# Message passing on 100,000 edges: seven edge splits in place of six, and who seeds and ends the last pass

## The chip, the cores and the metric

The kernel runs on 1 core of one Trainium2 chip. The metric is the device time of one execution in microseconds. Before the change it is 1114.98 us, the median of 3 runs (1113.57 to 1116.06). A profile was taken of one further execution; its times are counted from the first instruction.

## The reference

There are 6250 nodes with 128 features and 100,000 edges sorted by `dst`. Each edge makes a message from its two nodes and its own features, the messages are normed and cut at zero, and they are summed at `src` (which is in random order); then the nodes are normed.

```python
msg_in = concatenate([x[src], x[dst], edge_attr], axis=-1)      # 100000 x 384
h = msg_in @ W + b                                              # 100000 x 128
h = (h - mean(h)) * rsqrt(var(h) + 1e-5) * gamma + beta
msg = relu(h)
out = segment_sum(msg, src, num_segments=6250)
x = layernorm(x + out)
```

## The kernel before, in words

**Tiles and slots.** The edges are 782 tiles of 128. Four tiles make a *slot*; there are 196 slots, q = 0 to 195. The loop at the end of `fast_path` goes over the slots. In each slot TensorE forms the part of `h` that comes from the edge's features and from `x[dst]` (L619 and L623, into `hp`), ScalarE copies it out of the accumulators into a staging tile `hs` (`evict`, L633; a small copy at L568 adds one more column for three slots at a time), and GpSimd writes the tile's 128 rows into a table in HBM (`scatters`, L650), one indirect DMA for each tile, so 782 in all. The row to which an edge goes was worked out before by `places` (DVE, some TensorE and ScalarE work, in 20 pieces spread over the slots up to about 176). Staging has room for nine slots (`HS = 9`): ScalarE can be at most about that far ahead of GpSimd, and L568 is where it waits for room.

**Splits.** `scatters` sorts the edges by `src`: 50 blocks of 125 nodes. The edges come in splits, each with a table of its own in HBM. The list `SPLITS` holds for each split the number of tiles, k (each block has room for k x 128 edges), f (rows from f on are filled with neutral rows beforehand, `clear`, by DMAs from `empty`), and the sizes of the pieces of `places`. If a block of a split gets more than k x 128 or fewer than f edges, the program leaves the fast path for `general_path`. The number of tiles processed after sorting is 50 k for each split, filled or not.

**Items.** Once all edges of a split lie in its table, the split is taken in 25 pairs of blocks. An *item* is one pair (`n = 1`), or two pairs (`n = 2`, for splits with k = 2); an item has 2 k n tiles, handled in groups of at most four (k = 3: two groups of three; k = 4 and two-pair items: two groups of four; a single pair of k = 2: one group of four). For an item, `FLOW` lists these steps with an offset each: load `hl` (L725, SP), one-hot rows `ohe` (L748, DVE), their transposes (L760, TensorE) and the copy of them `ohn` (L764, ScalarE); for each group a copy of the rows into an accumulator (`seed`, L770, ScalarE), products that add `x[src]` (`pick`, L787, TensorE), squares (L796) and one root (L799) on ScalarE, a reciprocal (L805) and the norm with the cut at zero (L811) on DVE; for each pair the sums over edges (L820, TensorE, into `pa`) and their addition to `acc` (L826, DVE). Four work steps go with each item, so items follow each other at four steps' distance. `steps_due(q)` says how many steps are to have been done by slot q: the 25 items of a split are spread evenly over the slots between the end of that split plus 5 slots (`LAG`) and the end of the next split plus 5. The order on each engine is thus fixed in the program; GpSimd's scatters of a slot are tied to products of the following slot.

**The last split** has no later slots to hide behind. Its 25 pairs are taken as 14 *units* (sizes 1, eleven times 2, 1, 1) by the class `Unit` in `tail`, which also ends the nodes: `begin`, `stats`, `var`, `norm`, `end` give the final norm, and `end` issues the DMA that writes a unit's nodes out. A unit's `seed` is a product with the identity on TensorE (L876) or a copy on ScalarE (L874). The last four units a, b, c, d are ended by hand behind the loop. `end` takes two GpSimd instructions (L972, L973), or one DVE instruction for each block (L976) where its argument says so.

Of the kernel before, what the change touches and what calls it, by code (L numbers as in the profile page):

```python
# [12 lines left out]
AF = mybir.ActivationFunctionType  # L13
# [11 lines left out]
NB, BN = 50, 125  # L25
# [10 lines left out]


SPLITS = [(168, 4, 320, [12, 24, 44, 44, 44]),
          (168, 4, 320, [42, 42, 42, 42]),
          (168, 4, 320, [42, 42, 42, 42]),  # L40
          (120, 3, 192, [40, 40, 40]),
          (80, 2, 128, [40, 40]),
          (78, 2, 128, [39, 39])]
EARLY = 19
TMAX = 44
BY_PE = 4
# [24 lines left out]
def col_bc(t, n):  # L71

    return t.unsqueeze(2).to_broadcast([t.shape[0], t.shape[1], n])
# [7 lines left out]
def flat(t):  # L81
    return t.rearrange("p t d -> p (t d)")


def fast_path(ctx, tc, io, bad_d, found):
# [3 lines left out]
    nc = tc.nc  # L89
# [157 lines left out]
    bias = const.tile([P, D], F32, name="bias")  # L247
# [587 lines left out]
    class Unit:  # L835
# [130 lines left out]
            nc.vector.scalar_tensor_tensor(self.shift[:, :m], self.total[:, :m], -1.0 / D,  # L966
                                           self.frstd[:, :m], op0=ALU.mult, op1=ALU.mult)

        def end(self, last=False):
            y, m = self.y, self.m  # L970
            if not last:
                nc.gpsimd.tensor_tensor(y, y, col_bc(self.frstd[:, :m], D), op=ALU.mult)  # L972
                nc.gpsimd.tensor_tensor(y, y, col_bc(self.shift[:, :m], D), op=ALU.add)  # L973
            else:
                for j in range(m):
                    nc.vector.tensor_scalar(y[:, j, :], y[:, j, :], self.frstd[:, j:j + 1],  # L976
                                            self.shift[:, j:j + 1], op0=ALU.mult, op1=ALU.add)
            nc.sync.dma_start(io["out"][:, self.b0 * D:(self.b0 + m) * D], flat(y))


    n_split = len(SPLITS)
# [95 lines left out]
    TWINS = 8  # L1077
    pairs, first_item = [], []
    for s in range(n_split - 1):
        n = TWINS if s == n_split - 2 else 0  # L1080
        first_item.append(len(pairs))
        pairs += [(s, p, 2) for p in range(0, 2 * n, 2)]
        pairs += [(s, p, 1) for p in range(2 * n, NB // 2)]
# [31 lines left out]
    def work(n):  # L1115

        nonlocal n_steps
        for _ in range(n):
            for off, step in FLOW:
                i = n_steps - LEAD - off  # L1120
                if i % 4 or not 0 <= i // 4 < len(pairs):
                    continue
                if step is None:
                    load_pairs(*pairs[i // 4])
                    continue
                if off == 0:
                    at_work[i // 4] = Pairs(i // 4, *pairs[i // 4])
                step(at_work[i // 4])
            n_steps += 1
# [9 lines left out]
    def steps_due(q):  # L1139
        for (q0, n0), (q1, n1) in zip(due, due[1:]):  # L1140
            if q0 <= q < q1:
                return n0 + (n1 - n0) * (q - q0) // (q1 - q0)
        return 0
# [12 lines left out]
    for s, (n_tiles, _, _, _) in enumerate(SPLITS):  # L1156
        p0, p1 = first_tile[s] // PT, -(-first_tile[s + 1] // PT)
        slots = p1 - p0
        for i in range(slots):
# [16 lines left out]
            n = steps_due(q + 1) - n_steps  # L1176
# [25 lines left out]
    units = [Unit(sum(sizes[:i]), n) for i, n in enumerate(sizes)]  # L1202
    n = len(units)
# [49 lines left out]
    work(1)  # L1253
    units[0].turned()
    work(1)
    units[0].pick(0)
    units[1].ones()
    work(2)
    units[1].turn()
# [12 lines left out]
    a, b, c, d = units[-4:]  # L1272
# [21 lines left out]
    c.var()  # L1294
    for u in (b, d, c):
        u.norm()
        u.end(u is not b)
    order.close()


@with_exitstack
def gnn_resnorm_kernel(ctx, tc, io):
    nc = tc.nc
    keep = ctx.enter_context(tc.tile_pool(name="keep", bufs=1))
    bad_t = keep.tile([1, 1], I32, name="bad_t")
    with ExitStack() as inner:
        found = []
        fast_path(inner, tc, io, bad_t, found)
    with tc.If(found[0] > 0, preferred_fallthrough_block=True, label="general"):
        with ExitStack() as inner:  # L1310
            general_path(inner, tc, io)
# [233 lines left out]
```

## Time and profile before

| | |
|---|---|
| median of the runs | 1114.98 us |
| the profiled execution's own time | 1118.29 us |
| its span, first to last instruction | 1116.5 us |
| mean granted TensorE clock | 0.904 of full speed |
| busy: TensorE / DVE / ScalarE / GpSimd | 868.9 / 846.0 / 754.6 / 798.5 us |
| moved by DMA | 247.20 MB, 221 GB/s over the span |

A row of a timeline has the start in us, the duration in us, the engine, the line, the operation, output <- inputs, the shape, the count, and in brackets the idle time of the engine just ahead of it with what ended that. In a table by windows each row has the window, its length, the busy time of the engine with the number of instructions, then the granted clock, the share of the DMA engines and GB/s. In a table of waits, the numbers are the total in us, how often, and the longest. The names of engines are PE (TensorE), DVE (VectorE), ACT (ScalarE), POOL (GpSimd) and SP (SyncE); L650 is a line of the kernel above. "issue" is idle time for which the profile shows no wait.

### The profile page before, as it was taken

Reading aid. Unit: us, or ns where it says so; the run is one execution under the profiler, and the core shown is the slowest. Engines: PE = TensorE matmul, PEld = TensorE weight load, DVE = VectorE, ACT = ScalarE, POOL = GpSimd, SP = SyncE. Lnnn points to the kernel's source line nnn. Section 1 sums busy time; section 2 is a strip of 40 time slices with the busy share of each in tenths; the row PEclk is TensorE's granted clock in tenths of the full one; section 3 lists DMA queues with packets and bytes.
Section 4 is the critical chain, followed back from the end, with each engine's and each line's share of the span. In section 5 each row is a group of like instructions: output and inputs, shape, how many; then the busy total and the mean of one; then the engine's idle time right before and its main releaser. Section 6 shows DMA issues by size and latency. Waiting matters only on the chain. (4 is left out here: it accounts for less than half of the span.)

```text
span 1116.5 us, 27245 instructions
## 1 busy us (share of the span) xinstructions
PE 868.9 (78%) x8880; PEld 805.1 (72%) x8880; DVE 846.0 (76%) x2364; ACT 754.6 (68%) x2983; POOL 798.5 (72%) x832
## 2 busy tenths in 40 slices
PE   6758656454887688788868688888989899987994
PEld 3657546444887678788868688887978788976773
DVE  7874656634687587768777687988898988877997
ACT  4324422115776667567767678887988999987995
POOL 2677777777777777777777777777777777774264
PEclk7788897666999899878989899998999999999998
DMA  7799999546787666667877648876877767744331
GB/s 218 230 274 267 287 312 295 185 157 205 246 282 223 218 207 204 224 205 242 277 236 239 209 147 290 268 228 223 256 245 241 232 200 248 250 144 136 124 122 61
DMA packets 128050, 247.20 MB, mean 221 GB/s; under 512 B 47005, under 2 KB 61231, under 8 KB 127897
## 3 DMA queue, kind: packets, MB, share of 16 engines
q1 hardware_dynamic: 101924, 191.92, 56.0%
q0 software_dynamic: 25104, 53.05, 13.3%
q8 instruction: 71, 1.16, 0.5%
q14 instruction: 81, 0.66, 0.2%
q10 hardware_dynamic: 870, 0.40, 0.1%
HBM read 155.49 MB, written 89.80 MB: 220 GB/s over the span
## 5 line engine op out<-in xcount | busy, mean ns | idle before, releaser
L650 POOL DMA_INDIRECT sorted<-hs,place_i x782 | 758.1, 969 | 251.0 <-issue 94.2
L787 PE MATMUL sel<-xa,ohn 128*128 128x128 bf16 x2550 | 189.1, 226 | 107.1 <-ACT sel L770 105.9
L619 PE MATMUL hp<-w,eT 128*128 128x128 f32 x1564 | 240.5, 303 | 22.0 <-ACT hs L633 22.0
L619 PEld LDWEIGHTS hp<-w,eT 128*128 128x128 f32 x1564 | 218.7, 214 | 53.0 <-issue 27.2
L787 PEld LDWEIGHTS <-ohn 128*128 128x128 bf16 x2550 | 165.4, 101 | 118.3 <-issue 99.8
L811 DVE SCALAR_TENSOR_TENSOR msg<-sel,rstd,cut 128x128 f32<-128x128 f32 x850 | 240.5, 345 | 7.9
L820 PE MATMUL pa<-msg,ohe 128*128 128x130 f32 x1700 | 231.3, 288 | 15.3 <-DVE acc L826 8.6
L796 ACT ACTIVATE sq<-sel 128x128 f32<-128x128 f32 x850 | 224.4, 282 | 27.8 <-PE sel L787 27.6
L820 PEld LDWEIGHTS pa<-msg,ohe 128*128 128x128 f32 x1700 | 210.8, 199 | 20.2 <-DVE acc L826 10.2
L796 ACT ACTIVATION_READ_ACCUMULATOR sq<-sel 128x1 f32 x850 | 180.9, 213 | 0.0
L748 DVE TENSOR_TENSOR ohe<-hl,beside 128x1024 f32<-128x1024 f32 (+2 forms) x117 | 130.2, 1113 | 21.4 <-DMA hl<-sorted 10.5
L633 ACT COPY hs<-hp 128x512 f32<-128x512 f32 x196 | 113.4, 580 | 43.5 <-PE hp L623 36.5
L770 ACT COPY sel<-hl 128x512 f32<-128x512 f32 (+1 forms) x225 | 128.1, 569 | 15.9 <-DVE msg L811 15.6
L568 ACT COPY hs<-sloc 128x12 f32<-128x12 f32 x66 | 14.1, 213 | 161.3 <-DMA sorted<-hs,place_i 158.7
L607 DVE TENSOR_SCALAR ohd<-db,part_w 128x512 bf16<-128x512 bf16 x192 | 69.1, 361 | 61.4 <-DMA db<-drel_d 47.2
L764 ACT COPY ohn<-tr 128x1024 bf16<-128x1024 bf16 (+2 forms) x117 | 107.8, 921 | 5.3 <-PE tr L760 5.3
L805 DVE RECIPROCAL rstd<-std 128x4 f32<-128x4 f32 (+1 forms) x225 | 38.2, 170 | 80.8 <-ACT std L799 79.7
L826 DVE TENSOR_TENSOR acc<-acc,pa 128x260 f32<-128x260 f32 x125 | 52.3, 418 | 54.4 <-PE pa L820 54.3
L623 PE MATMUL hp<-win,ohd 126*128 126x128 bf16 x782 | 82.0, 231 | 1.1 <-DMA win<-xb_d 1.1
L799 ACT ACTIVATE std<-ss,eps 128x4 f32<-128x4 f32 (+1 forms) x225 | 66.9, 297 | 7.3
L760 PE MATMUL tr<-ident_h,ohe 128*128 128x128 bf16 x850 | 69.4, 225 | 2.4 <-issue 2.0
L623 PEld LDWEIGHTS <-ohd 126*128 126x128 bf16 x782 | 66.2, 105 | 5.1 <-issue 1.4
(199 smaller groups left out, 1033.9 us busy)
## 6 DMA issues: line engine op xcount, KB each, us to landing
eT<-in_eT SPq DMA_DIRECT2D x96, 512.0 KB
hl<-sorted SPq DMA_DIRECT2D x75, 528.0 KB
db<-drel_d SPq DMA_DIRECT2D x96, 256.0 KB
sorted<-empty SPq DMA_DIRECT2D x100, 198.0 KB
hl<-sorted SPq DMA_DIRECT2D x50, 264.0 KB
sorted<-hs,place_i POOLq DMA_INDIRECT x782
hl<-sorted SPq DMA_DIRECT2D x25, 396.0 KB
sorted<-empty SPq DMA_DIRECT2D x50, 132.0 KB
```

The lines of the kernel that those rows point to most:

```text
L619: pe(nc.tensor.matmul(hp[:, j, :], eT[:, at], w[:, 2, :], start=j == 0, stop=False, skip_group_check=True), 4)
L623: pe(nc.tensor.matmul(hp[:, j, :], oh[:3 * WN, at], win[:3 * WN, :], start=False, stop=j == m - 1, skip_group_check=True))
L633: nc.scalar.copy(hs[:, :m, 0:D], hp[:, :m, :])
L650: i = nc.gpsimd.indirect_dma_start(out=sorted_d[s][:, :], out_offset=bass.IndirectOffsetOnAxis(ap=place_i[:parts, t:t + 1], axis=0), in_=h ...
L748: nc.vector.tensor_tensor(self.ohe[:, :k, :], self.hl[:, :k, D:D + 1].to_broadcast([P, k, P]), row_bc(iota_p, k), op=ALU.is_equal)
L760: pe(nc.tensor.transpose(tr[:, j, :], half[:, j0 + j, 1::2], ident_h))
L764: nc.scalar.copy(self.ohn[:, :self.k, :], self.tr[:, :self.k, :])
L770: nc.scalar.copy(self.sel[g][:, :m, :], self.hl[:, j0:j0 + m, 0:D])
L787: pe(nc.tensor.matmul(sel[:, j, :], self.ohn[:, j0 + j, :], xa[:, b, i * D:(i + 1) * D], start=False, stop=j == m - 1 and i == 2, skip_gro ...
L796: nc.scalar.activation(sq[:, j, :], self.sel[g][:, j, :], AF.Square, accum_out=ss[:, j:j + 1])
L811: nc.vector.scalar_tensor_tensor(self.msg[:, j0 + j, 0:D], self.sel[g][:, j, :], rstd[:, j:j + 1], cut, op0=ALU.mult, op1=ALU.max)
L820: pe(nc.tensor.matmul(self.pa[:, h, :], self.ohe[:, i * k + j, :], self.msg[:, i * k + j, :], start=(j == h), stop=(j == k - 2 + h)), 4)
```

## The change

The list of splits has seven entries. The sum of k over the splits is 19 in both versions, the last split has k = 2 in both, and so 850 sorted tiles are taken as items and 100 as units in both. The fifth split (k = 2) is taken as twelve two-pair items and one single; the sixth, like the fifth before, as eight two-pair items and nine singles. There are 130 items in place of 117 and 250 groups in place of 225. The first unit's seed moves from TensorE to ScalarE. Of the last three units, b is ended by DVE in place of GpSimd, d by ScalarE in place of DVE, and c by DVE as before.

```diff
 SPLITS = [(168, 4, 320, [12, 24, 44, 44, 44]),
-          (168, 4, 320, [42, 42, 42, 42]),
-          (168, 4, 320, [42, 42, 42, 42]),
-          (120, 3, 192, [40, 40, 40]),
+          (124, 3, 192, [42, 42, 40]),
+          (124, 3, 192, [42, 42, 40]),
+          (124, 3, 192, [42, 42, 40]),
           (80, 2, 128, [40, 40]),
-          (78, 2, 128, [39, 39])]
+          (80, 2, 128, [40, 40]),
+          (82, 2, 128, [42, 40])]
...
-        def end(self, last=False):
+        def end(self, last=None):
             y, m = self.y, self.m
-            if not last:
+            if last is nc.scalar:
+                for j in range(m):
+                    nc.scalar.activation(y[:, j, :], y[:, j, :], AF.Identity,
+                                         bias=self.shift[:, j:j + 1],
+                                         scale=self.frstd[:, j:j + 1])
+            elif last is None:
                 nc.gpsimd.tensor_tensor(y, y, col_bc(self.frstd[:, :m], D), op=ALU.mult)
                 nc.gpsimd.tensor_tensor(y, y, col_bc(self.shift[:, :m], D), op=ALU.add)
             else:
...
-        n = TWINS if s == n_split - 2 else 0
+        n = 0 if SPLITS[s][1] > 2 else TWINS if s == n_split - 2 else NB // 4
...
-    units[0].pick(0)
+    units[0].pick(0, nc.scalar)
...
     for u in (b, d, c):
         u.norm()
-        u.end(u is not b)
+        u.end(nc.scalar if u is d else nc.vector)
```

How the items lie over the slots, from `steps_due` with each list (an item of n pairs has 2 k n tiles):

| before: slots | items of split | tiles a slot | after: slots | items of split | tiles a slot |
|---|---|---|---|---|---|
| 47 to 89 | 1st | 4.8 | 47 to 78 | 1st | 6.5 |
| 89 to 131 | 2nd | 4.8 | 78 to 109 | 2nd | 4.8 |
| 131 to 161 | 3rd | 6.7 | 109 to 140 | 3rd | 4.8 |
| 161 to 181 | 4th | 7.5 | 140 to 160 | 4th | 7.5 |
| | | | 160 to 180 | 5th | 5.0 |
| 181 to 190 | 5th, two-pair | 7.1 | 180 to 190 | 6th, two-pair | 6.4 |
| 190 to 197 | 5th, single | 5.1 | 190 to 197 | 6th, single | 5.1 |

The first place is ScalarE's queue between its copy of slot 173 into staging and that of slot 174, where `hs` is the staging tile, and `sel`, `sq` and `std` are the seed, squares and root of a group (the numbers are those of the buffers). Before the change:

```order
L770 COPY sel_12973<-hl_12689 128x384
L796 ACTIVATE sq_12976,ss_12975<-sel_12917 128x128 x3
L799 ACTIVATE std_12980<-ss_12975,eps_100 128x3
L764 COPY ohn_12956<-tr_12957 128x768
L770 COPY sel_13006<-hl_12783 128x384
L796 ACTIVATE sq_13009,ss_13008<-sel_12973 128x128 x3
L799 ACTIVATE std_13013<-ss_13008,eps_100 128x3
L770 COPY sel_13064<-hl_12783 128x384
L796 ACTIVATE sq_13067,ss_13066<-sel_13006 128x128 x3
L799 ACTIVATE std_13071<-ss_13066,eps_100 128x3
L568 COPY hs1_194<-sloc_164 128x12
L633 COPY hs1_194<-hp_13050 128x4x128
```

After the change, the same engine between the copies of the same two slots (its lines stand one further on):

```order
L765 COPY ohn_13566<-tr_13567 128x1024
L771 COPY sel_13644<-hl_13322 128x512
L797 ACTIVATE sq_13647,ss_13646<-sel_13606 128x128 x4
L800 ACTIVATE std_13652<-ss_13646,eps_101 128x4
L569 COPY hs1_197<-sloc_165 128x12
L634 COPY hs1_197<-hp_13669 128x4x128
```

Three groups of three tiles stood there between two slots, and one group of four stands there now; the other groups went to earlier slots.

The second place is the beginning of the last pass on ScalarE: `ohn` is the first unit's copied transposes, followed by the last item's squares. Before:

```order
L867 COPY ohn<-tr 128x512
L796 ACTIVATE sq,ss<-sel 128x128 x4
L799 ACTIVATE std<-ss,eps 128x4
L898 ACTIVATE sq,ss_15466<-sel 128x128 x4
L901 ACTIVATE std_15472<-ss_15466,eps 128x4
```

And now:

```order
L868 COPY ohn<-tr 128x512
L797 ACTIVATE sq,ss<-sel 128x128 x4
L800 ACTIVATE std<-ss,eps 128x4
L875 COPY sel<-hl 128x512
L899 ACTIVATE sq,ss_15856<-sel 128x128 x4
```

The seed stands behind the last item's squares and root, and the product L876 that made it is gone from TensorE's queue at that place.

The third place is the end of DVE's queue: `frstd` and `shift` belong to the final norm of b (4 blocks), d and c (2 each), in that order. Before:

```order
L964 RECIPROCAL frstd<-fstd 128x4
L966 TENSOR_SCALAR shift<-total,frstd 128x4
L964 RECIPROCAL frstd<-fstd 128x2
L966 TENSOR_SCALAR shift<-total,frstd 128x2
L976 TENSOR_SCALAR y<-y,frstd,shift 128x128 x2
```

And now:

```order
L965 RECIPROCAL frstd<-fstd 128x4
L967 TENSOR_SCALAR shift<-total,frstd 128x4
L982 TENSOR_SCALAR y<-y,frstd,shift 128x128 x4
L965 RECIPROCAL frstd<-fstd 128x2
L967 TENSOR_SCALAR shift<-total,frstd 128x2
```

DVE's four instructions for b come in ahead of d's norm, and d's two leave DVE: ScalarE's queue now ends with them (L974).

## The prediction

> **What bounds the kernel now.** I read the engines' totals first, then GpSimd's scatters by stretch, then ScalarE's waits for staging, then the table by stages, then the last 15 us. The totals point at no engine:
>
> ```profile
> PE 868.9 (78%) x8880; PEld 805.1 (72%) x8880; DVE 846.0 (76%) x2364; ACT 754.6 (68%) x2983; POOL 798.5 (72%) x832
> ```
>
> The scatters, taken by their line in two stretches, tell more (duration min/median/max in ns, then first and last start):
>
> ```profile
> L650 POOL DMA_INDIRECT sorted<-hs,place_i x481: 963/967/1128, 277.5 to 889.0; - x161
> L650 POOL DMA_INDIRECT sorted<-hs,place_i x102: 868/967/1068, 890.3 to 1024.4; - x102
> ```
>
> In the first stretch 480 intervals take 611.5 us, 1.274 us each, with hardly a deviation: GpSimd goes at its own pace, 5.10 us for a slot of four, and sets the time. In the second, 101 intervals take 134.1 us; at 1.274 they would take 128.7. So GpSimd lost **5.4 us** after 890 us, and the timeline says where and to whom:
>
> ```profile
> 908.41 0.97 POOL L650 DMA_INDIRECT sorted<-hs,place_i  x1 [1.92 <-PE pa L820]
> ...
> 1005.57 0.97 POOL L650 DMA_INDIRECT sorted<-hs,place_i  x1 [0.96 <-ACT sq L796]
> ...
> 1010.08 0.97 POOL L650 DMA_INDIRECT sorted<-hs,place_i  x1 [2.28 <-PE pa L820]
> ...
> 1024.40 0.87 POOL L650 DMA_INDIRECT sorted<-hs,place_i  x1 [0.30 <-issue]
> ```
>
> The usual gap is 0.30; here the other engines were late with what the scatters wait for. Behind the last scatter stand its landing, the loads of the first units, and a dense last pass:
>
> ```profile
> 1026.54 15.29 SPq L847 DMA_DIRECT2D hl<-sorted  x13
> 1029.23 0.69 DVE L854 TENSOR_TENSOR ohe<-hl,beside 128x512 f32<-128x512 f32 x1 [0.95 <-DMA hl<-sorted]
> ```
>
> ```profile
> 1050.00:1100.00 50.00, 48.31 (x459) 37.25 (x458) 48.34 (x209) 45.84 (x243) 30.05 (x29) 1.00 0.30 101
> ```
>
> DVE waits for the data at 1029.23, so the pass starts when the scatters let it; after that PE and DVE are busy 48 us in 50. The program therefore has two parts: scatters until 1025.3 (1024.40 + 0.87), then 91.2 us to the span's end at 1116.5, with 100 tiles in both versions.
>
> Why was GpSimd starved only late? ScalarE's waits for staging room, in 240 to 440, 440 to 655 and 655 to 830 us, one row each (there is no such row from 830 to 945):
>
> ```profile
> ACT hs L568 <- DMA sorted<-hs,place_i: 53.9, 11, 14.7
> ...
> ACT hs L568 <- DMA sorted<-hs,place_i: 52.5, 14, 6.2
> ...
> ACT hs L568 <- DMA sorted<-hs,place_i: 2.8, 2, 2.0
> ```
>
> and the copies into staging (x is slots) in the stages:
>
> ```profile
> 240.00:440.00 200.00, 21.75 (x38) 0.87 0.74 237
> 440.00:655.00 215.00, 24.83 (x43) 0.89 0.71 226
> 655.00:830.00 175.00, 18.54 (x32) 0.98 0.74 238
> 830.00:945.00 115.00, 11.57 (x20) 1.00 0.72 228
> 945.00:990.00 45.00, 5.20 (x9) 1.00 0.74 239
> 990.00:1018.00 28.00, 2.32 (x4) 1.00 0.38 110
> ```
>
> By the counts these are the first to fourth splits' items, then the two-pair items and the singles. The engines' own need for a slot is the window less the wait, over the slots: (200 - 53.9)/38 = 3.84 us and (215 - 52.5)/43 = 3.78 at 4.8 tiles a slot; (175 - 2.8)/32 = 5.4 at 6.7 tiles; 115/20 = 5.75 at 7.5; 45/9 = 5.0 at 7.1; 28/4 = 7.0 for the singles. Against GpSimd's 5.10, the first two stages have over a microsecond a slot to spare and the third and fourth are too slow. The engines enter 655 us with staging full, lose 32 x 0.3 = 10 us and, up to the stall at 908, some 14 slots x 0.65 = 9 us. A full lead is thus worth about **19 us** of falling behind.
>
> **The change part by part.** *The splits.* The 850 tiles before the last pass stay, and the dense end thins: slots 131 to 190 had 6.7, 7.5 and 7.1 tiles a slot, slots 109 to 190 get 4.8, 7.5, 5.0 and 6.4. By the needs above (between 3.8 at 4.8 tiles and 5.4 at 6.7 I take 5.2 for 6.5): slots 47 to 78 lose 31 x 0.1 = 3 us of lead, 78 to 140 win it back at over 1 us a slot, 140 to 160 lose 20 x 0.65 = 13 us of the 19, 160 to 180 win about 20 x 1.1, again full. The two-pair stage is no denser than the 5.0 us one of before; the singles lose 7 x 1.9 = 13 us, and that too is within the 19. So no stall after 890 us should remain: between 0 and -5.4 us. I take **-5.0**, near the full end, since 13 of 19 leaves room only if the lead is really full.
>
> What the split adds: 25 more groups and 25 more additions, and groups of three in place of four.
>
> ```profile
> L770 ACT COPY sel<-hl 128x512 f32<-128x512 f32 x175 | 103.9, 594 | 13.7 <-DVE msg L811 13.7
> L770 ACT COPY sel<-hl 128x384 f32<-128x384 f32 x50 | 24.2, 484 | 2.2 <-DVE msg L811 2.0
> L799 ACT ACTIVATE std<-ss,eps 128x4 f32<-128x4 f32 x175 | 52.1, 297 | 5.7
> L805 DVE RECIPROCAL rstd<-std 128x4 f32<-128x4 f32 x175 | 29.7, 170 | 75.2 <-ACT std L799 74.9
> L826 DVE TENSOR_TENSOR acc<-acc,pa 128x260 f32<-128x260 f32 x125 | 52.3, 418 | 54.4 <-PE pa L820 54.3
> ```
>
> ScalarE: seeds 100 x 0.594 + 150 x 0.484 = 132.0 against 128.1, and 25 roots x 0.297 = 7.4, so 11 us; DVE: 25 x (0.418 + 0.170) = 14.7 us. Spread over 150 slots this is 0.1 us a slot, hidden by the microsecond to spare in slots 78 to 140 and 160 to 180; in the dense stage the need of 5.75 already has groups of three. Without that cover it would be up to 15 us. Fills grow by 25 DMAs of 132 KB and loads by 25 issues on SP: 3.3 MB beside 247.2, in stages whose DMA share is 0.71 to 0.74. I take 0.
>
> *The last three units.*
>
> ```profile
> 1106.69 0.17 DVE L966 SCALAR_TENSOR_TENSOR shift<-total,frstd 128x4 f32<-128x4 f32 x1
> 1107.03 0.17 DVE L964 RECIPROCAL frstd<-fstd 128x2 f32<-128x2 f32 x1 [0.17 <-ACT fstd L958]
> 1107.23 0.56 DVE L966 SCALAR_TENSOR_TENSOR shift<-total,frstd 128x2 f32<-128x2 f32 x1
> 1107.83 1.40 DVE L976 TENSOR_SCALAR y<-y,frstd,shift 128x128 f32<-128x128 f32 x2
> 1109.15 0.15 DVE L964 RECIPROCAL frstd<-fstd 128x2 f32<-128x2 f32 x1
> 1109.60 0.60 DVE L976 TENSOR_SCALAR y<-y,frstd,shift 128x128 f32<-128x128 f32 x2
> ```
>
> ```profile
> 1107.85 1.04 POOL L973 TENSOR_TENSOR y<-y,shift 128x512 f32<-128x512 f32 x1
> ```
>
> d's two instructions took 1.40 us and c's 0.60: while POOL works on b (to 1108.89), DVE is slow. With b on DVE, four instructions from 1106.86 take 1.2 us, the norms of d and c 0.45 each (1109.15 to 1109.60), c's two 0.60: 1109.55 in place of 1110.20. ScalarE's two for d come from 1108.5; such an operation is not in the trace, its bounds are nothing and the 0.33 us step at which L976 goes times two plus a start, under c's end either way. The DMA of c is then late next. Between 0 and -1.0; I take **-0.7**. Nothing is queued behind d's instructions on ScalarE.
>
> *The first unit's seed.*
>
> ```profile
> 1032.07 1.02 PE L876 MATMUL sel<-hl,ident 128*128 128x512 f32 x2
> 1032.08 0.30 ACT L799 ACTIVATE std<-ss,eps 128x4 f32<-128x4 f32 x1
> 1032.93 0.83 PE L887 MATMUL sel<-xa,ohn 128*128 128x128 bf16 x12
> ```
>
> It now waits behind that root: 1032.38 plus 0.59 for such a copy is 1032.97, where the picks began at 1032.93. Queued behind the picks on PE are the second unit's transposes and the last item's sums. Nothing won or lost: 0.
>
> *A cold restart of PE.* With a lead of 6 us or more at slot 195, PE has finished the items and stands idle some 7 us until the last scatters have landed; before, it was busy up to the end. What that costs shows at 250 us:
>
> ```profile
> 259.85 1.44 PE L787 MATMUL sel<-xa,ohn 128*128 128x128 bf16 x12 [11.15 <-ACT sel L770]
> 261.08 1.06 PE L760 MATMUL tr<-ident_h,ohe 128*128 128x128 bf16 x8
> 261.93 2.02 PE L619 MATMUL hp<-w,eT 128*128 128x128 f32 x8
> 265.00 1.14 PE L619 MATMUL hp<-w,eT 128*128 128x128 f32 x8
> 266.20 0.83 PE L787 MATMUL sel<-xa,ohn 128*128 128x128 bf16 x12
> ```
>
> After 11.15 us idle, twelve picks take 1.44 in place of 0.83 and eight f32 products 2.02 in place of 1.14; some 4 us later all is fast again. At the restart stand four transposes (+0.2), eight f32 sums (+0.9, half hidden, since PE no longer has the seed) and twelve picks (+0.6), ahead of an addition for which DVE waits. Between 0 and +2; I take **+1.0**. The Trainium skill, "TensorE: Matmul & The Clock Gate", section "What's actually happening", states that an idle window of about 3.4 us halves the clock and a busy one restores it, and the rows above agree (1.44 over 0.83, for about 4 us). By this rule alone any idle gap over 3.4 us ahead of the last pass costs the restart, and without it the sum below would be 1 us less.
>
> *Sum:* -5.0 - 0.7 + 0 + 1.0 = -4.7 us. The profiled execution took 1118.29 (its span 1116.5 and 1.8 around it), so it would take 1113.6; it lies 3.3 above the median of the runs, and the same step from the median gives 1114.98 - 4.7 = **1110.3 us**.
>
> **The rivals.** *The stall only moves.* The stage at 7.5 tiles a slot is still there, at slots 140 to 160. It needs 13 us of lead; if splits' beginnings keep the lead at slot 140 under that, GpSimd loses it there instead, and a scatter lost early is as lost as a late one. Against: 62 light slots stand ahead, and the waits of 53.9 and 52.5 show how much is spare at 4.8 tiles. Price: the 5.0 comes back, 1115.3; without the idle gap 1114.3. I call it 1114.5.
>
> *Slower, by slots 47 to 78.* They get 6.5 tiles a slot, where the clock was 0.87 in place of 0.98. The stage decides from 5.10 + 19/31 = 5.7 us a slot on. At 6.0 it loses 28 us, of which 19 are lead: 9 us of stall, 1110.3 + 9 = 1119. For it: PE's cold rows above stand just there. Against:
>
> ```profile
> 240.00:440.00 200.00, 148.66 (x1563) 143.12 (x1564) 141.22 (x362) 128.32 (x501) 152.13 (x158) 0.87 0.74 237
> ```
>
> PE had 148.66 us of work in these 200, and in the table of stages a busier engine goes with a higher clock.
>
> *A longer cold start.* If the gaps in the first units keep PE slow for 8 us, the +1.0 becomes 4: 1113.3.
>
> *The change doesn't run as said.* With a block over k x 128 the general path would run, many times slower. Counted from the reference's inputs, the fullest block of the new splits has 252 edges of 256 (the last split) and 364 of 384, and the emptiest are above f (163 against 128). I give it nothing.
>
> **How the numbers follow.** Forecast 0.67, stall moves 0.16, slower 0.10, long cold start 0.07. A measurement of this kernel tells about 0.2%, 2.2 us, from no change, so faster means under 1112.75 and slower over 1117.2. The forecast is faster nearly throughout; the moved stall is within 0.2%; the long cold start is half and half: faster 0.70, same 0.20, slower 0.10. Range: all terms at their better ends give -5.4 - 1.0 = -6.4, 1108.6, and 1 us is left for stalls before 890 us that I take as fixed (1107.5); upward it takes in the moved stall with an end that wins nothing (1114.98) and stops at 1115.5, which leaves the slower case out.
>
> **What will show it.** Right: the last 102 scatters at 1.274 to 1.28 us, no gap over 0.5 there; ScalarE waits for staging again in slots 78 to 140 and 160 to 190; the last scatter's end near 1020; the last pass's first picks at 1.4 and DVE's last instruction 0.7 sooner after the first `ohe`. Wrong: gaps of POOL at 290 to 420 us (slower) or 740 to 850 us (the stall moved), or staging waits that never come back after slot 140.

## The result and the profile after

The changed kernel takes **1110.81 us**, the median of 7 runs (1109.95 to 1111.81), beside 1115.53 for the kernel before on the same chip (7 runs): a ratio of 0.9955, with a 95% interval of 0.9944 to 0.9967. The forecast was 1110.3. The profiled execution took 1110.36 us, its span 1108.6.

The totals tell as little as before: each engine has a little more or less to do, and the span is shorter.

```profile
PE 865.3 (78%) x8878; PEld 799.1 (72%) x8878; DVE 858.5 (77%) x2436; ACT 767.3 (69%) x3049; POOL 796.4 (72%) x830
```

The scatters by their line in the same two stretches (duration min/median/max in ns, then first and last start):

```profile
L651 POOL DMA_INDIRECT sorted<-hs,place_i x481: 963/967/1108, 277.4 to 888.8; - x161
...
L651 POOL DMA_INDIRECT sorted<-hs,place_i x102: 867/967/1042, 888.8 to 1017.3; - x102
```

480 intervals in 611.4 us are 1.274 each, as before; and now the last 101 take 128.5 us, 1.272 each. The second stretch has lost its stalls entirely. ScalarE's waits for staging room, in 240 to 440, 440 to 700 and 700 to 830 us (there is no such row from 830 to 1020):

```profile
ACT hs L569 <- DMA sorted<-hs,place_i: 15.2, 8, 8.2
...
ACT hs L569 <- DMA sorted<-hs,place_i: 44.8, 13, 6.7
...
ACT hs L569 <- DMA sorted<-hs,place_i: 1.1, 1, 1.1
```

Staging is full up to about 714 us, slot 141, which is one slot into the dense stage. It is never full again. How near that comes to a stall is read from the **lead** of a slot: the start of its first scatter less the start of its copy into staging. These are the copy and the scatter of slot 141 and of slot 159, the first and the last of the dense stage, and the copies' window between them:

```profile
713.40 0.58 ACT L634 COPY hs<-hp 128x512 f32<-128x512 f32 x1
...
741.04 0.96 POOL L651 DMA_INDIRECT sorted<-hs,place_i  x1 [0.30 <-DMA sorted<-hs,place_i]
...
825.87 0.58 ACT L634 COPY hs<-hp 128x512 f32<-128x512 f32 x1
...
832.62 0.97 POOL L651 DMA_INDIRECT sorted<-hs,place_i  x1 [0.30 <-issue]
```

```profile
713.40:825.87 112.47, 10.41 (x18) 0.97 0.79 241
```

The lead goes from 27.6 to 6.8 us: 18 slots take 6.25 us each where GpSimd needs 5.09, and **20.8 us** are used. It comes back to 18.9 at slot 180 and 22.3 at 189, and the singles take it to 12.4.

The beginning of the last pass:

```profile
1017.30 0.87 POOL L651 DMA_INDIRECT sorted<-hs,place_i  x1 [0.30 <-issue]
...
1022.11 0.69 DVE L855 TENSOR_TENSOR ohe<-hl,beside 128x512 f32<-128x512 f32 x1 [8.23 <-DMA hl<-sorted]
...
1022.86 0.61 PE L865 MATMUL tr<-ident_h,ohe 128*128 128x128 bf16 x4 [7.57 <-DVE ohe L855]
...
1023.75 2.09 PE L821 MATMUL pa<-msg,ohe 128*128 128x130 f32 x8 [0.29 <-DVE msg L812]
...
1025.99 1.44 PE L888 MATMUL sel<-xa,ohn 128*128 128x128 bf16 x12
...
1028.99 0.43 DVE L827 TENSOR_TENSOR acc<-acc,pa 128x260 f32<-128x260 f32 x1 [1.31 <-PE pa L821]
```

DVE now waits 8.23 us for the data where it waited 0.95, and TensorE 7.57: everything else is done, and only the scatters set when the pass starts. After the wait the twelve picks take 1.44 us, where the profile before had 0.83 at this place, and the addition starts 6.88 us after `ohe`, where it was 1035.20 - 1029.23 = 5.97. The addition in the profile before:

```profile
1035.20 0.43 DVE L826 TENSOR_TENSOR acc<-acc,pa 128x260 f32<-128x260 f32 x1 [0.98 <-PE pa L820]
```

The table of the profile after by windows, with the granted clock behind POOL's busy time, says why:

```profile
1016.00:1020.00 4.00, 0.00 (x0) 0.00 (x0) 0.00 (x0) 0.00 (x0) 1.83 (x2) 0.66 0.12 38
1020.00:1024.00 4.00, 0.86 (x5) 0.62 (x6) 1.85 (x6) 0.50 (x2) 0.00 (x0) 0.50 0.85 261
1024.00:1028.00 4.00, 3.85 (x29) 3.58 (x30) 3.15 (x9) 2.38 (x15) 0.00 (x0) 0.55 0.79 279
1028.00:1032.00 4.00, 3.85 (x45) 3.03 (x44) 2.98 (x8) 3.52 (x18) 0.00 (x0) 1.00 0.36 90
```

The clock falls to half in the idle time and is back at 1028. And the end of the kernel:

```profile
1100.61 1.11 DVE L982 TENSOR_SCALAR y<-y,frstd,shift 128x128 f32<-128x128 f32 x4
...
1102.02 0.88 ACT L974 ACTIVATE y<-y,shift,frstd 128x128 f32<-128x128 f32 x2 [0.22 <-DVE shift L967]
1102.38 0.60 DVE L982 TENSOR_SCALAR y<-y,frstd,shift 128x128 f32<-128x128 f32 x2
```

Where the time went, by the two profiles:

| piece | before | after | difference |
|---|---|---|---|
| start of the first scatter of slot 14 | 95.18 | 93.78 | -1.40 |
| lost by GpSimd, slots 14 to 170 (over 1.272 a scatter) | 1.35 | 1.28 | -0.07 |
| lost by GpSimd, slots 170 to 195 | 5.67 | 0.04 | **-5.63** |
| end of the last scatter to the first `ohe` | 3.96 | 3.94 | -0.02 |
| first `ohe` to DVE's last instruction's end | 80.98 | 80.87 | -0.11 |
| from there to the end of the span | 6.29 | 5.62 | -0.67 |
| span | 1116.5 | 1108.6 | -7.9 |

The profiles differ by 7.9, the medians by 4.7: the profiled execution of before lies 2.8 above its median (1118.29 to 1115.53), that of after 0.5 below. The other two profiles with six splits, in the experiments below, are also of the slowest execution of their runs. So the 5.2 to 7.2 us that these three profiles show lost behind slot 170 need not be lost in a median execution.

### The profile page after: what moved, and what is told of

Same layout as the page of the kernel before. It is cut to its first block, busy times and chain, and to the rows that moved or that the text cites. A ratio compares the mean times of both kernels' runs of the same rounds, so it can differ in the third digit from the quotient of the medians.

```text
span 1108.6 us, 27458 instructions
## 1 busy us (share of the span) xinstructions
PE 865.3 (78%) x8878; PEld 799.1 (72%) x8878; DVE 858.5 (77%) x2436; ACT 767.3 (69%) x3049; POOL 796.4 (72%) x830
## 5 line engine op out<-in xcount | busy, mean ns | idle before, releaser
L651 POOL DMA_INDIRECT sorted<-hs,place_i x782 | 758.1, 969 | 243.3 <-issue 96.6
L821 PE MATMUL pa<-msg,ohe 128*128 128x130 f32 x1700 | 237.1, 288 | 30.8 <-DVE acc L827 22.8
L812 DVE SCALAR_TENSOR_TENSOR msg<-sel,rstd,cut 128x128 f32<-128x128 f32 x850 | 243.0, 345 | 8.8
L749 DVE TENSOR_TENSOR ohe<-hl,beside 128x768 f32<-128x768 f32 (+2 forms) x130 | 132.2, 1017 | 36.8 <-PE beside L503 21.3
L771 ACT COPY sel<-hl 128x384 f32<-128x384 f32 (+1 forms) x250 | 132.1, 529 | 19.9 <-DVE msg L812 19.2
L765 ACT COPY ohn<-tr 128x768 bf16<-128x768 bf16 (+2 forms) x130 | 109.6, 843 | 5.9 <-PE tr L761 5.9
L827 DVE TENSOR_TENSOR acc<-acc,pa 128x260 f32<-128x260 f32 x150 | 62.8, 419 | 51.9 <-PE pa L821 51.6
L800 ACT ACTIVATE std<-ss,eps 128x3 f32<-128x3 f32 (+1 forms) x250 | 74.2, 297 | 8.1
L806 DVE RECIPROCAL rstd<-std 128x3 f32<-128x3 f32 (+1 forms) x250 | 42.3, 169 | 46.7 <-ACT std L800 44.5
```

The source lines that it names most:

```text
L651: i = nc.gpsimd.indirect_dma_start(out=sorted_d[s][:, :], out_offset=bass.IndirectOffsetOnAxis(ap=place_i[:parts, t:t + 1], axis=0), in_=h ...
L749: nc.vector.tensor_tensor(self.ohe[:, :k, :], self.hl[:, :k, D:D + 1].to_broadcast([P, k, P]), row_bc(iota_p, k), op=ALU.is_equal)
L765: nc.scalar.copy(self.ohn[:, :self.k, :], self.tr[:, :self.k, :])
L771: nc.scalar.copy(self.sel[g][:, :m, :], self.hl[:, j0:j0 + m, 0:D])
L800: nc.scalar.activation(std[:, :m], ss[:, :m], AF.Sqrt, bias=eps, scale=1.0 / D)
L812: nc.vector.scalar_tensor_tensor(self.msg[:, j0 + j, 0:D], self.sel[g][:, j, :], rstd[:, j:j + 1], cut, op0=ALU.mult, op1=ALU.max)
```

## The experiments

The theory is the prediction's: the thinner end lets ScalarE keep a lead in staging, so that GpSimd no longer starves behind 890 us; the three hand-made ends win a little; and TensorE, idle before the last pass, starts it cold. The rivals: that the ends bring the gain; that more staging would have done as well; that the cold start eats more.

| run | median | before, same chip | ratio, 95% interval | lost, slots 170 to 195 | first `ohe` to DVE's end |
|---|---|---|---|---|---|
| before | | | | 5.67 | 80.98 |
| after | 1110.81 | 1115.53 | 0.9955, 0.9944 to 0.9967 | 0.04 | 80.87 |
| the splits alone | 1112.42 | 1116.29 | 0.9965, 0.9953 to 0.9978 | 0.40 | 82.15 |
| seed and ends alone | 1115.0 | 1116.29 | 0.9985, 0.9975 to 0.9994 | 5.16 | 80.08 |
| before, larger staging | 1115.07 | 1116.29 | 0.9985, 0.9974 to 0.9997 | 7.18 | 80.95 |
| after, TensorE kept busy | 1111.55 | 1116.29 | 0.9956, 0.9942 to 0.997 | 0.28 | 80.51 |
| after, old seed | 1114.03 | 1117.09 | 0.9971, 0.996 to 0.9981 | 0.18 | 81.48 |
| after, old ends | 1113.95 | 1117.09 | 0.9971, 0.9959 to 0.9983 | 0.30 | 81.83 |
| after, smaller staging | 1127.36 | 1117.09 | 1.0089, 1.0074 to 1.0104 | 2.89 | 80.09 |
| after, larger staging | 1113.11 | 1117.09 | 0.9965, 0.9952 to 0.9978 | 0.36 | 81.13 |
| a stage of ten tiles | 1131.95 | 1115.16 | 1.0147, 1.013 to 1.0164 | 0.16 | 81.60 |

**The splits alone.** The changed kernel with the old seed and the old ends:

```diff
-    units[0].pick(0, nc.scalar)
+    units[0].pick(0)
...
-        u.end(nc.scalar if u is d else nc.vector)
+        u.end(None if u is b else nc.vector)
```

> Only the list of splits with its two-pair items; the seed and the ends are those of before. Theory (GpSimd no longer starves after 890 us, and TensorE restarts cold): the last 102 scatters go at 1.27 us each with no gap over 0.5 us, the time falls by about 3 us against before: 5.4 won, 1.0 lost to the cold restart, and another 1 because the seed's two products now run cold ahead of the picks. Rival (the gain is made at the end, and the splits only move work): no difference to before.

Measured: 3.9 us less than before (interval 2.5 to 5.2). The stalls behind 890 us are gone, and the last pass takes 82.15 us from its first `ohe`, 1.17 more than before, with nothing of its own changed: that is the cold start. With these 1.2 put back, the splits win about 5 in front of the last pass by the times as well; the 1.4 us before slot 14 in the table above are part of it.

**Seed and ends alone.** The kernel before with the new seed and ends, its own splits and items:

```diff
 SPLITS = [(168, 4, 320, [12, 24, 44, 44, 44]),
-          (124, 3, 192, [42, 42, 40]),
-          (124, 3, 192, [42, 42, 40]),
-          (124, 3, 192, [42, 42, 40]),
+          (168, 4, 320, [42, 42, 42, 42]),
+          (168, 4, 320, [42, 42, 42, 42]),
+          (120, 3, 192, [40, 40, 40]),
           (80, 2, 128, [40, 40]),
-          (80, 2, 128, [40, 40]),
-          (82, 2, 128, [42, 40])]
+          (78, 2, 128, [39, 39])]
...
-        n = 0 if SPLITS[s][1] > 2 else TWINS if s == n_split - 2 else NB // 4
+        n = TWINS if s == n_split - 2 else 0
```

> Only the seed on ScalarE and the three ends, with the six splits of before. Theory: 0.7 us less than before, all of it behind the first one-hot rows of the last pass; the stalls of GpSimd at 908 and 1010 us stay. Rival (the gain is made at the end): 4 to 5 us less.

Measured: 1.7 us less (0.7 to 2.8), of which the last pass shows 0.90, and the stalls stand where they stood, almost to the microsecond:

```profile
908.15 0.97 POOL L650 DMA_INDIRECT sorted<-hs,place_i  x1 [1.38 <-PE pa L820]
...
1009.82 0.97 POOL L650 DMA_INDIRECT sorted<-hs,place_i  x1 [2.28 <-PE pa L820]
```

So the splits, and only they, remove the stalls, and they are the larger part of the gain.

**More staging for the kernel before.** Ten slots of room in place of nine (tiles of two slots each, not three):

```diff
-    HS, HG = 9, 3
+    HS, HG = 10, 2
```

> The kernel before with room for ten slots in staging, in groups of two, in place of nine in groups of three; nothing else. Theory (ScalarE's lead over GpSimd is what is used up): the lead grows by one to two slots, 5 to 10 us, so GpSimd no longer starves and the time falls by 3 to 4 us with the old splits: 5.4 won, up to 2 lost to a cold restart. Rival (the old splits' dense stage holds up the scatters whatever the lead, or the new splits win by something else): within 1 us of before.

This missed: not 3 to 4 us less but 1.7 (0.3 to 2.9), and 7.18 us lost behind slot 170, not fewer. The ratio is that of the run before, so the times alone do not tell the two apart; the stalls do. ScalarE's lead did rise, to between 33 and 42 us in the light stages. But from slot 133 to slot 134, soon behind the slot at which the third split's items begin (131), it fell from 39.7 to 27.7 us, and in the kernel before from 30.3 to 27.9: behind this place the two are alike. The waits of that place (655 to 700 us) of SP for the last scatters of the split, and of DVE for the load behind them:

```profile
SPq L725 <- DMA sorted<-hs,place_i: 20.7, 1, 20.7
...
DVE ohe L748 <- DMA hl<-sorted: 10.7, 1, 10.7
```

In the kernel before SP's wait at this place is shorter:

```profile
SPq L725 <- DMA sorted<-hs,place_i: 12.0, 1, 12.0
```

A split's first item needs that split's last scatters. ScalarE, further ahead of GpSimd, reaches the item sooner in its queue and waits there the longer. A split's boundary cuts the lead back to what `LAG` leaves, 5 slots of 5.1 us. More room cannot carry a lead across it; only items that lie elsewhere can change what is needed behind it.

**TensorE kept busy.** 28 products into an unused accumulator ahead of the last pass, read by nobody:

```diff
+    warm_up(28)
     units[0].turn()
```

> The changed kernel with 28 idle products of 128 x 512 on TensorE ahead of the first unit's transposes, about 6 of its 7.6 us of idling. Theory (the restart is cold and DVE waits for it): the first picks of the last pass take 0.83 us in place of 1.44, the time from the first one-hot rows to DVE's second addition behind them falls from 6.9 to 6.0 us, and the time by 0.9 against the changed kernel, 5.6 against before. Rival (PE's speed there is hidden behind DVE): no difference to the changed kernel.

Measured: no different from the changed kernel (0.9956 to 0.9955), and 0.36 us less in the last pass, not 0.9. TensorE's rows and its windows:

```profile
1015.21 6.21 PE L1010 MATMUL hp<-ones_h 128*128 128x512 bf16 x28
1023.65 0.40 PE L865 MATMUL tr<-ident_h,ohe 128*128 128x128 bf16 x4 [2.23 <-DVE ohe L855]
...
1026.58 1.26 PE L888 MATMUL sel<-xa,ohn 128*128 128x128 bf16 x12
```

```profile
1020.00:1024.00 4.00, 1.77 (x11) 0.67 (x9) 1.10 (x3) 0.00 (x0) 0.00 (x0) 1.00 0.66 213
1024.00:1028.00 4.00, 3.59 (x27) 3.32 (x27) 3.65 (x11) 2.48 (x12) 0.00 (x0) 0.57 0.81 276
```

Only 2.23 us were idle, the transposes ran at full speed (0.40), and then the clock fell all the same, while TensorE was busy again. In narrower windows the clock is 0.50 from 1024.1 to 1027.5. So the filling made the slow stretch shorter, 3.4 us in place of 10.2, and did not avoid it.

**The old seed.** The changed kernel with the first unit's seed on TensorE again:

```diff
-    units[0].pick(0, nc.scalar)
+    units[0].pick(0)
```

> The changed kernel with the first unit's seed on TensorE again. Theory (the restart is cold, so the seed's two products cost twice and stand ahead of the picks): 0.6 to 1.5 us slower than the changed kernel, with 7.5 to 8.4 us in place of 6.9 from the first one-hot rows to DVE's second addition. Rival (neutral, as the rows of before have it with a warm engine): no difference.

The last pass is 0.61 us longer (by the times 0.9971 in place of 0.9955, with intervals that overlap). The seed, the picks behind it and the addition that waits for the sums:

```profile
1021.97 0.69 DVE L855 TENSOR_TENSOR ohe<-hl,beside 128x512 f32<-128x512 f32 x1 [9.74 <-DMA hl<-sorted]
...
1025.51 1.79 PE L877 MATMUL sel<-hl,ident 128*128 128x512 f32 x2
...
1027.13 0.83 PE L888 MATMUL sel<-xa,ohn 128*128 128x128 bf16 x12
...
1029.40 0.43 DVE L827 TENSOR_TENSOR acc<-acc,pa 128x260 f32<-128x260 f32 x1 [1.97 <-PE pa L821]
```

At the low clock this seed takes 1.79 us, not the 1.02 of the profile before, and the addition comes 7.43 us after `ohe`, against 6.88 with ScalarE's seed. The difference of two profiles does not show what the seed is worth, since the moment at which the clock comes back differs between them as well; the step on the cold restart, below, has the numbers.

**The old ends.** The changed kernel with b on GpSimd and d on DVE:

```diff
-        u.end(nc.scalar if u is d else nc.vector)
+        u.end(None if u is b else nc.vector)
```

> The changed kernel with b ended by GpSimd and d and c by DVE, as before. Theory (DVE is slow while GpSimd works on b): 0.7 us slower than the changed kernel, with d's two instructions at about 1.4 us again. Rival (the end is set by the output's DMAs): no difference.

The last pass is 0.96 us longer. Where TensorE stays warm, it takes 80.98 and 80.95 with the old ends and 80.08 and 80.09 with the new (the table's rows of before, and of before with larger staging, against seed and ends alone, and after with smaller staging). GpSimd's second instruction for b and DVE's for d and c:

```profile
1101.77 1.04 POOL L979 TENSOR_TENSOR y<-y,shift 128x512 f32<-128x512 f32 x1
```

```profile
1101.74 1.40 DVE L982 TENSOR_SCALAR y<-y,frstd,shift 128x128 f32<-128x128 f32 x2
...
1103.52 0.60 DVE L982 TENSOR_SCALAR y<-y,frstd,shift 128x128 f32<-128x128 f32 x2
```

DVE's pair for d takes 1.40 beside GpSimd and 0.60 alone, as in the kernel before.

**Less staging.** The changed kernel with room for six slots, to take the lead away:

```diff
-    HS, HG = 9, 3
+    HS, HG = 6, 3
```

> The changed kernel with room for six slots in staging in place of nine. Theory (the new splits' dense stage at slots 140 to 160 lives on the lead): the lead's upper end falls from 26 to about 12 us, the stage uses up 20, so GpSimd starves between 740 and 850 us and again at the single items, and the time grows by 12 to 18 us against the changed kernel. Rival (the dense stage was not near the limit): under 3 us.

Measured: 1.0089, 15 us more than the changed kernel by the two ratios. At slot 141 the lead is 10.2 us where the changed kernel has 27.6, and the dense stage starves GpSimd at 773 to 848 us. The longest gap of that stretch:

```profile
813.41 0.97 POOL L651 DMA_INDIRECT sorted<-hs,place_i  x1 [2.79 <-PE pa L821]
```

17.2 us are lost up to slot 170 where the changed kernel loses 1.3, with the splits, items and instructions otherwise as they are (some 2 us of it because a scatter comes every 1.275 us here, the rest chiefly gaps in the dense stage). The lead is what covers the dense stage.

**More staging for the changed kernel.**

```diff
-    HS, HG = 9, 3
+    HS, HG = 10, 2
```

> The changed kernel with room for ten slots in staging, in groups of two. Theory: GpSimd does not starve after slot 13 already, so a larger lead wins nothing; within 1 us of the changed kernel. Rival (more staging helps by itself, not through the stalls): 2 us or more less than the changed kernel.

No gain, 0.9965: the lead rose to 38.6 us at slot 141 (27.6 without the tenth slot) and was 24.1 at slot 144, much as without it (22.9). The split's boundary cuts it here too: in 700 to 760 us SP waits 18.8 us for the split's last scatters, where it waits 11.1 in the changed kernel.

**Other orders of the splits.** Three lists with the sum of k still 19:

| | tiles of the splits in `SPLITS` |
|---|---|
| the changed kernel | 168, 124, 124, 124, 80, 80, 82 |
| first order | 168, 168, 124, 80, 80, 80, 82 |
| second order | 168, 124, 80, 124, 124, 80, 82 |
| third order | 168, 168, 80, 124, 80, 80, 82 |

A split of 168 tiles has k = 4, one of 124 k = 3, the others k = 2, each with the sizes of pieces that it has in the lists of the change.

> The changed kernel with the same kinds of splits in another order and number: 168, 168, 124, 80, 80, 80 and 82 tiles. The items lie at 4.8 tiles a slot up to slot 89, 6.5 in 89 to 120, 7.5 in 120 to 140, then 5.0. Account of the lead: the changed kernel kept its lead at 6.5 tiles and used 20.8 us of some 26 in a stage of 20 slots at 7.5, so here too it just suffices: no more than 2 us lost in all, the last scatters at their own pace, and 3 to 5 us less than before. Rival, that a dense stage must have a light one straight ahead of it, so that the lead is full: the lead at slot 120 is under 18 and 5 us or more are lost in slots 125 to 142, no gain over before.

> Splits of 168, 124, 80, 124, 124, 80 and 82 tiles: two dense stages of 7.5 tiles a slot, at slots 78 to 98 (straight behind 6.5) and 160 to 180 (behind 3.2 and 4.8), 31 slots of 3.2 between them. Account of the lead: each uses 21 us of 26, and the lead is won back between them, so up to slot 180 at most 2 us are lost. At slot 180 only some 5 us of lead are left, the two-pair items keep them and the singles need 10: some 3 to 5 us lost behind slot 190, and the last pass without its idle gap (-1). Together 1 to 3 us less than before. Rival, that every dense slot costs time whatever the lead: 20 x 1.05 = 21 us more than the changed kernel.

> Splits of 168, 168, 80, 124, 80, 80 and 82 tiles: the second split's 200 tiles fall into 20 slots, 89 to 109, at 10 tiles a slot. By the changed kernel's 6.15 us a slot at 7.5 tiles and 3.8 at 4.8 such a slot needs 6.15 + 2.5 x 0.87 = 8.3 us, 20 slots use 20 x (8.3 - 5.1) = 64 us, of which 26 are lead: 38 us lost in slots 95 to 109, all for good although 31 slots of 3.2 tiles follow; the dense stage at slots 140 to 160 is covered again, and the end is as in the changed kernel. So some 33 us more than before, between 20 and 45. Rival, that light slots behind give it back: under 10 more than before.

These three say nothing of the lead. They ran where the kernel before took 1363 us (the record numbers the chip 0, as for the first four experiments, in which it took 1116; why it was slower is not known). The scatters themselves lasted as long as ever there, but GpSimd stood idle for twice as long ahead of them, much of it with no wait that the profile shows. This is the group of the third order, where the changed kernel's has 758.1 busy and 243.3 idle:

```profile
L651 POOL DMA_INDIRECT sorted<-hs,place_i x782 | 760.5, 972 | 507.7 <-issue 177.2
```

The ratios were 1.0071, 1.0021 and 1.0164; whether the first two orders gain where the kernel before takes 1115 us stays open.

**A stage of ten tiles.** The third order once more, on a chip where the kernel before takes 1115.16:

> Splits of 168, 168, 80, 124, 80, 80 and 82 tiles once more, on a chip where the kernel before takes its usual 1115 us: 10 tiles a slot in slots 89 to 109, behind 4.8 and ahead of 3.2. By the account of the lead such a slot needs 8.3 us, 20 slots use 64 us, 26 of them lead: 38 us lost in slots 95 to 109 and not given back by the light slots behind, no loss at slots 140 to 160 nor behind 890 us; so some 33 us more than before, between 20 and 45. Rival, that light slots behind give it back: under 10 us more than before.

Measured: 1.0147, or 16.8 us more than before, at 0.16 lost behind slot 170. That is under the 20 to 45 that was expected, and over the rival's 10. The lead tells where the estimate was off. Copy and scatter of slots 90, 108 and 123, and the windows of slots 90 to 108 and 141 to 159:

```profile
452.66 0.58 ACT L634 COPY hs<-hp 128x512 f32<-128x512 f32 x1
...
480.52 0.97 POOL L651 DMA_INDIRECT sorted<-hs,place_i  x1 [0.31 <-issue]
...
583.04 0.58 ACT L634 COPY hs<-hp 128x512 f32<-128x512 f32 x1
...
589.56 0.96 POOL L651 DMA_INDIRECT sorted<-hs,place_i  x1 [0.30 <-ACT sel L771]
...
638.29 0.58 ACT L634 COPY hs<-hp 128x512 f32<-128x512 f32 x1
...
666.04 0.97 POOL L651 DMA_INDIRECT sorted<-hs,place_i  x1 [0.30 <-issue]
```

```profile
452.66:583.04 130.38, 10.37 (x19) 0.99 0.74 242
730.57:847.61 117.04, 10.39 (x19) 0.97 0.76 233
```

Ten tiles need 130.38 / 18 = 7.24 us a slot, not 8.3, so 18 slots fall 38.8 us behind 5.09. The lead gives 27.9 - 6.5 = 21.4 of it, and the other 17.4 are stall: the scatters' gaps from 530 to 587 us, over the usual 1.272, add up to 17.3. Fifteen slots later the lead is 27.8 us again, and GpSimd has won back nothing: **a scatter lost early stays lost.** In the later dense stage the lead fell to 5.7 us at slot 159, and there 3.7 us were lost; the changed kernel, whose lead ended at 6.8, lost none. So about 21 us of a lead of 27 can be used: while GpSimd waits for others in these stages, the lead still stands at 5 to 9 us.

## Why the prediction was right, step by step

**The splits: -5.0 forecast, -5.63 in the profiles.** Right in size and mechanism: the splits alone remove the stalls, the old splits keep them with everything else new, and taking the lead away brings 15 us of stalls. The full lead of 19 us was right too: about 21 can be used. But **the step "140 to 160 lose 20 x 0.65 = 13 us of the 19" was mis-sized.** The stage used 20.8 us, 6.25 us a slot in place of 5.75. The 5.75 was the mean of a window, 830 to 945 us of the kernel before, over two parts with different needs. The copies of slots 160 to 173 and of 173 to 181 there, and the scans of `places` on DVE in the same two windows:

```profile
817.87:899.08 81.21, 7.50 (x13) 1.00 0.72 230
899.08:943.27 44.19, 4.64 (x8) 1.00 0.69 224
```

```profile
817.87:899.08 81.21, 6.65 (x3) 1.00 0.72 230
899.08:943.27 44.19, 0.00 (x0) 1.00 0.69 224
```

While pieces of `places` were still being worked on, a slot took 81.21 / 13 = 6.25 us; without them 44.19 / 8 = 5.52. In the new dense stage two pieces lie, with four scans:

```profile
L456 DVE TENSOR_TENSOR_SCAN sc<-oh,sc,beside 128x1000 f16<-128x1000 bf16 (+1 forms) x2 | 4.7, 2340 | 0.0
...
L456 DVE TENSOR_TENSOR_SCAN sc<-oh,beside 128x1000 f16<-128x1000 bf16 (+1 forms) x2 | 4.6, 2284 | 0.0
```

There a slot took 6.25 again. So the right price stood in the trace before the change. That `places` makes the difference, by long instructions on DVE that items queue behind, fits these numbers and is argued: no run took it away, and the tiles of a slot, the clock and the DMA share differ somewhat between the stretches too.

The steps beside this one erred as well. Slots 47 to 78 were to lose 3 us of lead and kept it, at 24 to 28 us from slot 51 on. Slots 160 to 180 were to win 22 us, "again full", and won 12.4 (6.5 to 18.9): a sign that the prediction gave for being wrong, staging waits that never come back after slot 140, came true, and still nothing was lost, since the stages behind need little lead. That the stage found room was a near thing, and in part luck: in the run with the stage of ten tiles the lead fell to 5.7 at the same place, a microsecond lower, and the first rival, the moved stall, began there.

**What the split adds: 0 forecast.** It held as a sum: nothing is lost in slots 78 to 140, though ScalarE and DVE each have over 12 us more to do (767.3 against 754.6, 858.5 against 846.0). In the dense stage its part of the half microsecond a slot was not taken apart.

**The ends: -0.7 forecast, about -0.9 measured.** Up to DVE's last instruction they are worth 0.96 (old ends put back, 81.83 to 80.87) or 0.90 (seed and ends alone, 80.08 to 80.98), and the pairs with a warm TensorE agree within 0.03. From there to the end of the span it is 5.9 to 6.3 us in the four profiles with the old ends and 5.6 to 6.0 in the seven with the new, leaving out the three runs where the kernel before took 1363 us; these overlap, so the 0.67 of the table above is not shown to be the ends' work. ScalarE's pair, which no row of before showed, takes 0.88 us and ends at 1102.90, just under c's 1102.98: the upper bound of the prediction (0.66 and a start) was the right end.

**The seed: 0 forecast.** Right on a warm TensorE: the addition that waits for the first unit's sums starts 5.96 and 5.97 us after the first `ohe` with the old seed (before, and before with larger staging), 6.16 and 5.94 with the new (seed and ends alone, and after with smaller staging). On a cold one the old seed costs something. In the table below the addition comes the later, the later the clock comes back; a line through the four rows with ScalarE's seed gives 6.4 and 6.7 for the moments of the two rows with TensorE's seed, which have 7.11 and 7.42. So the new seed is worth about 0.7 there, an estimate from these six rows. The forecast weighed the seed and the cold start apart, though the second follows from the first term and changes the worth of the seed.

**The cold restart: +1.0 forecast, 0.8 to 1.5 measured.** With the seed on TensorE it costs 1.17 (the splits alone to before) to 1.40 (old seed, 81.48, to the 80.08 of the warm kernel with the new ends). With the seed on ScalarE the same instructions take 80.87, 81.13 and 81.60 in three profiles, so 0.79, 1.05 and 1.52. What differs is the moment at which the clock comes back. It is 0.50 for 10.2 us in each of these profiles, and for 13.7 us in the one of larger staging:

| run | seed by | slow clock ends, after first `ohe` | addition starts, after first `ohe` | ends | last pass |
|---|---|---|---|---|---|
| the splits alone | TensorE | 4.45 | 7.11 | old | 82.15 |
| after, old seed | TensorE | 5.07 | 7.42 | new | 81.48 |
| after | ScalarE | 5.45 | 6.88 | new | 80.87 |
| after, old ends | ScalarE | 6.15 | 7.21 | old | 81.83 |
| after, larger staging | ScalarE | 6.58 | 7.42 | new | 81.13 |
| a stage of ten tiles | ScalarE | 7.62 | 7.92 | new | 81.60 |

The windows around the end of the slow clock in the last of these, whose first `ohe` is at 1042.91:

```profile
1040.30:1050.52 10.22, 6.43 (x40) 5.92 (x41) 5.10 (x14) 4.57 (x21) 0.00 (x0) 0.50 0.71 240
1050.54:1054.00 3.46, 3.46 (x42) 2.89 (x42) 3.13 (x8) 2.29 (x15) 0.00 (x0) 1.00 0.34 94
```

So the +1.0 was the right size, but not a fixed price: it moves by 0.7 us from one profile to the next with the same instructions in the last pass. The rule of the Trainium skill, "TensorE: Matmul & The Clock Gate", section "What's actually happening", that an idle window of about 3.4 us halves the clock, agrees with the 7.57 us gap and the 0.50 of the windows. It does not tell the whole, since in the run with TensorE kept busy a gap of 2.23 us was followed by 3.4 us at 0.50. The rival of a longer cold start, 8 us of slow clock and +4, came near in its premise (7.62 us in the stage of ten tiles) but not in its price (1.52).

**What was not foreseen: -1.4 us before slot 14.** The profiles with seven splits reach slot 14 some 72.5 to 74.7 us after the first scatter, those with six after 74.2 to 75.7. The scatters and copies of these slots are the same in both; what DVE prepares for the splits beside them differs a little (`room` and `bkt`). No run tried it, and the ranges overlap, so the cause and even the gain stay open.

**Slower by slots 47 to 78** fell by the lead that stayed: in 250 to 395 us ScalarE waits 11.2 us for room over 27 slots, so a slot needed (145 - 11.2) / 27 = 5.0 us, where 5.2 was forecast and 6.0 feared. The clock there was 0.95, not the 0.87 of before; that this is the reason was not tried.

**The sum.** -4.7 was forecast and the medians show -4.7, with an interval by the ratio of -3.7 to -6.2. That the two agree to a tenth is luck: the profiles differ by 7.9, of which 1.4 have no known cause and part is the slow execution that was profiled.

## What to carry to other kernels

Where a fixed-pace engine sets the time, measure how far ahead of it the others are, stage by stage; a stage that is too dense costs only what exceeds that lead, and what it costs is not won back by light stages behind it. More buffer helps only as far as no dependence cuts the lead back: here each split's first item needs the split's last scatter, and a tenth slot of staging took no stall away. Where a stage's need is read from a window, see first that the window holds one kind of work. A change that lets an engine go idle before a serial tail changes the price of what stands in that tail, so cost the two together.

## What the runs showed of the hardware

A scatter of 128 rows that waits for nobody keeps its pace: the median from one start to the next is 1.272 to 1.276 us in all fourteen profiles, some 0.97 busy and 0.30 gap. That holds also where the kernel before took 1363 us, though a quarter of the intervals there are over 1.85.

TensorE's clock does not follow its idle time at once. With 6.21 us of filling and only 2.23 us idle, the first transposes still ran at full speed, and the clock then fell to 0.50 for 3.4 us while the work was going on (0.57 in the window of 4 us); 0.43 us of the cold start's price (80.51 to 80.08) was paid although the gap was short. Filling until the data arrive was not tried.

The slow stretches ahead of the last pass last 3.4, 10.2 or 13.7 us, which are 1, 3 and 4 times 3.4, and end 4.5 to 7.6 us after the first work, not at a fixed distance from it.
